# Cross-attention on one core: the first loads exchanged between two DMA queues, one quarter of x2 loaded ahead of Wq and Wk, nine warming products for ten

## The chip, the core and the metric

The kernel runs on one NeuronCore of a Trainium2 chip. Five engines work side by side, each through its own list of instructions: TensorE (PE, with its weight loads shown apart as PEld), VectorE (DVE), ScalarE (ACT), GpSimd (POOL) and SyncE (SP). Loads from HBM are issued by SP, ACT or POOL and are carried out by 16 DMA engines that all of them share. The metric is the time of one execution on the device in microseconds; smaller is better. A time is given as the median of several runs.

## What is computed

Eight batches. For each, with x1 and x2 of 512 channels by 1024 positions:

```python
q = jnp.einsum('bcn,dc->bnd', x1, Wq) + bq
k = jnp.einsum('bcn,dc->bdn', x2, Wk) + bk[:, None]
v = jnp.einsum('bcn,dc->bdn', x2, Wv) + bv[:, None]
attn = jax.nn.softmax(jnp.einsum('bnd,bdm->bnm', q, k), axis=2)
attn_out = jnp.einsum('bcm,bnm->bcn', v, attn)
return attn_out + x1
```

Wq and Wk have 64 rows, Wv has 512. All is float32.

## The kernel before

**How exact products are made.** Most large products are not done in plain float32. An operand is split into a high part (`h`, rounded by the float32r type), a low part (`l`) and a mixed one (`d`); three cheap products with these parts are then summed. For Wv the parts are made by `wh`, `wl`, `wd` and `w4`, for a quarter of x2 (256 positions, called a chunk) by `xh`, `xl`, `xd`. A few products are done in plain float32, since there is no time to split yet: those of v for the first quarter of x2 (`VF`, line 366), and the projections to q and k (`Q` and `K`, through `project`, line 205).

**What sets the order.** Nothing is scheduled by the compiler: three tables of words, `FIRST`, `MIDDLE` and `LAST`, list every step of a batch, and `follow` issues them in that order. Each engine takes its own steps out of that one list, in order. `FIRST` holds batch 0 and parts of batch 1, `MIDDLE` is used for batches 1 to 6. Ahead of them stands `begin` (line 515).

**The head.** `begin` issues, alternately, four pieces of the first quarter of x2 (`hx`, lines 163 to 166, 128 KB each, from SP) and four pieces of Wv (`hw`, lines 168 to 171, 256 KB each, from ACT). While these are on their way PE runs products on a tile of zeros, in three groups of four, three and three (`ps_warm`, line 525), and ACT evaluates one exponential, before which its table is loaded (line 528). Then `FIRST` starts:

```python
VF.0.0 VF.1.0 VF.1.1 wh.0 VF.1.2 VF.1.3 wl.0 wd.0 w4.0 wh.1 wl.1 wd.1 w4.1 VF.0.1 VF.0.2 VF.0.3 lwq ldx2.0
ldx2.1 xh.1 lsd K xl.1 xh.2 xh.3 ldx1.0 bv ke xd.1 xl.2 xl.3 VX.2 ldx1.1 jf.0 xd.2 xd.3 sy.2 sy.3 sy.5 jf.1 Q
```

`VF.j.c` is one float32 product of block j with piece c of x2's first quarter and piece c of Wv. `lwq` loads Wq and Wk (one tile, `wqk_sb`, 256 KB) and then the two biases (`bqk_sb`, 1 KB). `ldx2.0` loads the second quarter of x2 (512 KB), `ldx2.1` the second half (1024 KB), `lsd` the bias of v, and each `ldx1` two pieces of x1 of 512 KB; all of these are issued by SP. `K` needs all of x2 and Wk: its products alternate between the first half of x2 and the second, piece by piece. `VX.2` comes right behind it on PE, then `Q`, which needs x1.

**How loads wait for one another.** The framework gives the loads that SP and ACT issue eight completion semaphores in turn (`DMAHW0` to `DMAHW7`). A load that takes a semaphore again waits until the load that had it before, the eighth before it in the order of issue, has landed. A queue issues in order, so whatever stands behind such a load waits with it.

Of the kernel before, what the change touches and what calls it, by code (L numbers as in the profile page):

```python
# [10 lines left out]
FR = mybir.dt.float32r  # L11
AF = mybir.ActivationFunctionType
ALU = mybir.AluOpType
# [10 lines left out]
T = 4096.0  # L24
SPLIT = 1.0 - 2.0**-13
# [2 lines left out]


FIRST = """  # L30
VF.0.0 VF.1.0 VF.1.1 wh.0 VF.1.2 VF.1.3 wl.0 wd.0 w4.0 wh.1 wl.1 wd.1 w4.1 VF.0.1 VF.0.2 VF.0.3 lwq ldx2.0
ldx2.1 xh.1 lsd K xl.1 xh.2 xh.3 ldx1.0 bv ke xd.1 xl.2 xl.3 VX.2 ldx1.1 jf.0 xd.2 xd.3 sy.2 sy.3 sy.5 jf.1 Q
kc VY.2 VY.3 qe kr cy.2 cy.3 vh.0 qd kl jn.2 vl.0 qr sy.4 VX.3 jn.3 vh.1 VX.4 VY.5 cy.5 vd.0 VX.5 VY.4 cy.4 ql
S.0.0 S.0.1 S.0.2 S.0.3 S.0.5 Sc.0.0 Sc.0.1 Sc.0.2 Sc.0.3 S.0.4 Sc.0.4 Sc.0.5 S.0.6 Sc.0.6 S.0.7 Sc.0.7 S.1.1
# [48 lines left out]
def kernel(  # L83
# [12 lines left out]
    nc = tc.nc  # L96
    P = 128
    B, N, C = x1T.shape
    D = wqk.shape[3]
    CT = C // P  # L100
    MT = N // P
    H = 512
    QN = 256
# [8 lines left out]
    bqk_sb = const.tile([P, 2], F32, name="bqk_sb")  # L112
# [4 lines left out]
    wraw, wtmp = {}, {}  # L117

    BUFS = {"X": 3, "Y": 3, "sc": 2, "raw": 2, "top": 2, "kh": 5, "kl": 5, "kd": 4, "es": 2, "few": 2, "r": 2, "y": 2, "o": 3, "x": 2}

    LATE = (6, 7)

    def f32(t):
        return t.bitcast(F32)

    def new(shape, tag, name, dtype=F32):
        return sb.tile(shape, dtype, tag=tag, name=name, bufs=BUFS.get(tag, 1))

    def bank(tag, name):
        return psum.tile([P, H], F32, tag=tag, name=name, bufs=BUFS[tag])  # L130

    class Batch:
# [30 lines left out]
        def hx(self, c):  # L163
            if c == 0:
                self.x2[0] = new([P, 2, CT, QN], "x", "x2_0_0")
            nc.sync.dma_start(self.x2[0][:, 0, c, :], x2[0, :, 0, c])

        def hw(self, c):
            if c % 2 == 0:
                wraw[c // 2] = new([P, 2, C], "kd", f"w_raw{c // 2}")  # L170
            nc.scalar.dma_start(wraw[c // 2][:, c % 2, :], wvT[c])

        def lwq(self):
            nc.sync.dma_start(wqk_sb, wqk)
            nc.sync.dma_start(bqk_sb, bqk)

        def lsd(self):
            nc.sync.dma_start(seed, bv.broadcast_to([P, C]))
# [168 lines left out]
        def chunk(self, k):  # L347
            return self.x2[k // 2][:, k % 2]

        def xh(self, k):  # L350
            self.c[k] = {"h": new([P, CT, QN], "kh", f"xh_{self.b}_{k}", FR)}
            nc.scalar.activation(self.c[k]["h"], self.chunk(k), AF.Copy, scale=-SPLIT)

        def xl(self, k):
            self.c[k]["l"] = new([P, CT, QN], "kl", f"xl_{self.b}_{k}", FR)
            nc.vector.tensor_tensor(self.c[k]["l"], self.chunk(k), f32(self.c[k]["h"]), ALU.add)

        def xd(self, k):
            c = self.c[k]
            c["d"] = new([P, CT, QN], "kd", f"xd_{self.b}_{k}", FR)  # L360
            nc.vector.scalar_tensor_tensor(c["d"], f32(c["l"]), T, f32(c["h"]), ALU.mult, ALU.add)

        def VF(self, j, c):
            if c == 0:
# [101 lines left out]
        def late(self, u):  # L466
            return u in LATE and not self.final

# [46 lines left out]
    def begin():  # L515
        for c in range(CT):
            states[0].hx(c)
            states[0].hw(c)
        nc.vector.memset(warm, 0.0)
        nc.vector.memset(spark, 0.0)  # L520

        for i, times in enumerate((4, 3, 3)):
            ps = bank("Y", f"ps_warm{i}")
            for k in range(times):
                nc.tensor.matmul(
                    ps, warm, warm.unsqueeze(1).to_broadcast([P, 4, P]), start=(k == 0), stop=(k == times - 1)
                )
        nc.scalar.activation(spark, spark, AF.Exp)
# [10 lines left out]
    with tc.manual_schedule():  # L539
        begin()  # L540
        follow(FIRST, 0)
        for b in range(1, B - 1):
            follow(MIDDLE, b)
        follow(LAST, B - 1)
# [31 lines left out]
```

## Time and profile before

| what | value |
|---|---|
| median of 3 runs | 660.87 us (660.82 to 661.15) |
| the profiled execution | 661.69 us |
| its span, first to last instruction | 659.9 us |
| PE busy | 652.8 us, 99% of the span |
| DVE, ACT, POOL busy | 619.0, 452.4, 203.5 us |
| read from HBM, written to it | 51.91 MB, 16.78 MB |

The span covers the program's instructions; 1.8 us of the profiled execution lie around it. PE is busy nearly from end to end, so what can change is, above all, when it starts on useful work and where it still waits. The page's list of waits gives PE's own waits: 1.4 us for a load of x ahead of `K`, 1.0 us at the very start, 0.8 us and 0.2 us later for ACT.

### The profile page before, as it was taken

What the parts mean: (1) busy time and instruction counts of PE and PEld (TensorE: products, weight loads), DVE (VectorE), ACT (ScalarE), POOL (GpSimd) and SP (SyncE); (2) the same over time, 40 slices, a digit from 0 to 9 for tenths busy, and PEclk for the clock granted to TensorE, in tenths of its full rate; (3) what the DMA queues carried; (4) which work ended last, traced back from release to release, by engine and by line L of the source; (5) the groups of instructions that cost most, each with busy time, mean ns of one, the idle gap of its engine ahead of it and who ended that gap; (6) DMA issues with size and microseconds to landing.
All of it is one profiled execution on the core that took longest, in us unless ns stands there. A gap on an engine that the chain in (4) does not pass through costs nothing.

```text
span 659.9 us, 8059 instructions
## 1 busy us (share of the span) xinstructions
PE 652.8 (99%) x2802; PEld 492.4 (75%) x2802; DVE 619.0 (94%) x689; ACT 452.4 (69%) x670; POOL 203.5 (31%) x162
## 2 busy tenths in 40 slices
PE   8999999999999999999999999999999999999997
PEld 3664888677886688866888668886688776887886
DVE  4789999999999999999999999999999999999994
ACT  5688676876587675876767757677675975759542
POOL 0014432323414333043520335212352214412451
PEclk9999999999999999999999999999999999999999
DMA  8534648364665647474563745737367275632374
GB/s 316 191 96 107 119 98 221 73 201 96 129 175 112 175 98 163 124 173 120 114 173 96 216 100 111 173 83 224 81 128 179 77 207 98 126 81 49 93 150 124
DMA packets 41464, 90.21 MB, mean 137 GB/s; under 512 B 13136, under 2 KB 13904, under 8 KB 37712
## 3 DMA queue, kind: packets, MB, share of 16 engines
q0 software_dynamic: 13536, 33.04, 30.0%
q1 hardware_dynamic: 27312, 55.62, 25.4%
q10 hardware_dynamic: 576, 1.05, 0.4%
q8 instruction: 22, 0.36, 0.2%
q14 instruction: 18, 0.15, 0.1%
HBM read 51.91 MB, written 16.78 MB: 104 GB/s over the span
## 4 chain that ended last, share of the span: by engine, by line
PE 96%; DMA 2%; ACT 1%; DVEq 0%; issue 0%; ACTq 0%; DVE 0%
PE ps_oX L426 34%; PE ps_oY L426 17%; PE ps_vX L386 17%; PE ps_s L262 9%; PE ps_vY L386 8%; PE ps_k L205 4%; PE ps_q L205 4%; PE ps_o L451 2%; DMA x<-in_x_dram 1%; DMA w_raw<-in_wvT_dram 1%; ACT eh L297 0%; ACT e L293 0%; ACT ps_vY L382 0%; ACT vy L401 0%; ACT es L312 0%; ACT vh L408 0%
## 5 line engine op out<-in xcount | busy, mean ns | idle before, releaser
L426 PE MATMUL ps_oY<-vd,ed 128*128 128x512 f32 x496 | 193.2, 392 | 0.0
L426 PE MATMUL ps_oX<-vh,eh 128*128 128x512 f32 x496 | 193.0, 389 | 0.0
L426 PE MATMUL ps_oX<-vl,el 128*128 128x512 f32 x496 | 193.0, 389 | 0.0
L426 PEld LDWEIGHTS ps_oY<-vd,ed 128*128 128x128 f32 x496 | 93.1, 188 | 25.0 <-issue 5.1
L506 POOL DMA_DIRECT2D o<-in_x1T_dram x62 | 55.6, 916 | 171.6 <-ACT o L503 97.6
L426 PEld LDWEIGHTS ps_oX<-vl,el 128*128 128x128 f32 x496 | 93.1, 188 | 19.5
L426 PEld LDWEIGHTS ps_oX<-vh,eh 128*128 128x128 f32 x496 | 93.1, 188 | 19.3 <-issue 0.2
L293 ACT ACTIVATE e<-e 128x1024 f32<-128x1024 f32 x64 | 67.9, 1062 | 49.6 <-DVE e L290 48.3
L267 ACT COPY e<-ps_s 128x512 f32<-128x512 f32 x128 | 70.9, 589 | 28.6 <-PE ps_s L262 27.6
L329 POOL PARTITION_ALL_REDUCE den<-es x32 | 80.7, 2522 | 26.0 <-DVE es L319 25.0
L306 DVE SCALAR_TENSOR_TENSOR ed<-el,eh 128x1024 fp32r<-128x1024 f32 x62 | 83.0, 1341 | 2.1
L315 POOL DMA_DIRECT2D es<-e x32 | 28.6, 895 | 179.1 <-ACT es L312 166.9
L301 DVE TENSOR_TENSOR el<-e,eh 128x1024 fp32r<-128x1024 f32 x62 | 79.5, 1298 | 0.0
L290 DVE TENSOR_TENSOR e<-e,top 128x1024 f32<-128x1024 f32 x64 | 77.0, 1231 | 0.0
L282 POOL PARTITION_ALL_REDUCE top<-max x32 | 46.9, 1466 | 68.0 <-DVE max L278 67.9
L386 PE MATMUL ps_vX<-wh,xh 128*128 128x512 f32 x248 | 67.6, 394 | 0.0
L386 PE MATMUL ps_vY<-wd,xd 128*128 128x512 f32 x248 | 65.9, 393 | 0.8 <-ACT ps_vY L382 0.8
L386 PE MATMUL ps_vX<-wl,xl 128*128 128x512 f32 x248 | 66.3, 389 | 0.0
L297 ACT ACTIVATE eh<-e 128x1024 fp32r<-128x1024 f32 x62 | 64.6, 1054 | 0.5
L401 ACT COPY vy<-ps_vY 128x512 f32<-128x512 f32 x62 | 36.4, 591 | 40.0 <-PE ps_vY L386 38.8
L386 PEld LDWEIGHTS ps_vX<-wh,xh 128*128 128x128 f32 x248 | 45.8, 188 | 15.7 <-DVE max L277 4.1
L386 PEld LDWEIGHTS ps_vY<-wd,xd 128*128 128x128 f32 x248 | 46.2, 188 | 12.5 <-ACT ps_vY L382 1.6
(59 smaller groups left out, 963.5 us busy)
## 6 DMA issues: line engine op xcount, KB each, us to landing
x<-in_x_dram SPq DMA_DIRECT2D x29, 1024.0 KB, 6.6
es<-e POOLq DMA_DIRECT2D x32, 512.0 KB, 4.6
out_dram<-o SPq DMA_DIRECT2D x63, 256.0 KB, 2.4
o<-in_x1T_dram POOLq DMA_DIRECT2D x62, 256.0 KB, 4.3
x<-in_x_dram SPq DMA_DIRECT2D x5, 512.0 KB, 10.3
k<-k SPq DMA_DIRECT2D x16, 128.0 KB, 2.2
q<-q SPq DMA_DIRECT2D x16, 128.0 KB, 2.4
w_raw<-in_wvT_dram ACTq DMA_DIRECT2D x4, 256.0 KB, 4.1
```

Of the source, the lines that this page charges most:

```text
L205: nc.tensor.matmul(ps[r, :], wqk_sb[:, which, c, :], x(h, c), start=(c == 0), stop=(c == CT - 1))
L262: nc.tensor.matmul(ps, k[:, ts(i, P)], self.qa[:, ts(h, H)], start=(z == 0), stop=(z == 1))
L267: nc.scalar.copy(self.half[h][:, :, i, :], self.ps[h, i].rearrange("p (q n) -> p q n", q=2))
L290: nc.vector.tensor_tensor(e, e, top, ALU.subtract)
L293: nc.scalar.activation(self.unit(u), self.unit(u), AF.Exp)
L297: nc.scalar.activation(self.e[u]["h"], self.unit(u), AF.Copy, scale=SPLIT)
L301: nc.vector.tensor_tensor(self.e[u]["l"], self.unit(u), f32(self.e[u]["h"]), ALU.subtract)
L306: nc.vector.scalar_tensor_tensor(e["d"], f32(e["l"]), -T, f32(e["h"]), ALU.mult, ALU.add)
L329: nc.gpsimd.partition_all_reduce(self.den[Q], self.es[Q][:, 0, :], P, ReduceOp.add)
L386: nc.tensor.matmul(ps, self.c[j // 2][z][:, c, ts(j % 2, P)], w[z][:, c, :], start=(start and c == 0), stop=(stop and c == CT - 1), skip_g ...
L426: nc.tensor.matmul(ps, self.e[u][z][:, m, :], self.v[m // 2][z][:, m % 2, :], start=start, stop=stop, skip_group_check=True,)
L506: nc.gpsimd.dma_start(self.o[u], x1T[self.b, ts(u, P), :], accum_op=ALU.add)
```

## The change

Four things in the head of the program; every other step keeps its place.

- The pieces of x2's first quarter (`hx`) are issued by ACT, the pieces of Wv (`hw`) by SP.
- `ldx2.0` stands ahead of `lwq` in `FIRST`.
- The two biases leave `lwq` and are issued by ACT, right behind the pieces of x2.
- Nine warming products in three groups of three, for ten.

The functions `xh`, `xl` and `xd` now take the part of a chunk that `apart` gives. With `WHOLE = 2` its condition compares a chunk's number with 0.5, which no whole number equals, so that part is always the whole chunk and these instructions keep their shape of 128x1024.

```diff
@@ -28,7 +28,7 @@
 
 
 FIRST = """
-VF.0.0 VF.1.0 VF.1.1 wh.0 VF.1.2 VF.1.3 wl.0 wd.0 w4.0 wh.1 wl.1 wd.1 w4.1 VF.0.1 VF.0.2 VF.0.3 lwq ldx2.0
+VF.0.0 VF.1.0 VF.1.1 wh.0 VF.1.2 VF.1.3 wl.0 wd.0 w4.0 wh.1 wl.1 wd.1 w4.1 VF.0.1 VF.0.2 VF.0.3 ldx2.0 lwq
 ldx2.1 xh.1 lsd K xl.1 xh.2 xh.3 ldx1.0 bv ke xd.1 xl.2 xl.3 VX.2 ldx1.1 jf.0 xd.2 xd.3 sy.2 sy.3 sy.5 jf.1 Q
 kc VY.2 VY.3 qe kr cy.2 cy.3 vh.0 qd kl jn.2 vl.0 qr sy.4 VX.3 jn.3 vh.1 VX.4 VY.5 cy.5 vd.0 VX.5 VY.4 cy.4 ql
 S.0.0 S.0.1 S.0.2 S.0.3 S.0.5 Sc.0.0 Sc.0.1 Sc.0.2 Sc.0.3 S.0.4 Sc.0.4 Sc.0.5 S.0.6 Sc.0.6 S.0.7 Sc.0.7 S.1.1
@@ -118,6 +118,8 @@
 
     BUFS = {"X": 3, "Y": 3, "sc": 2, "raw": 2, "top": 2, "kh": 5, "kl": 5, "kd": 4, "es": 2, "few": 2, "r": 2, "y": 2, "o": 3, "x": 2}
 
+    WHOLE = 2
+
     LATE = (6, 7)
 
     def f32(t):
@@ -163,16 +165,15 @@
         def hx(self, c):
             if c == 0:
                 self.x2[0] = new([P, 2, CT, QN], "x", "x2_0_0")
-            nc.sync.dma_start(self.x2[0][:, 0, c, :], x2[0, :, 0, c])
+            nc.scalar.dma_start(self.x2[0][:, 0, c, :], x2[0, :, 0, c])
 
         def hw(self, c):
             if c % 2 == 0:
                 wraw[c // 2] = new([P, 2, C], "kd", f"w_raw{c // 2}")
-            nc.scalar.dma_start(wraw[c // 2][:, c % 2, :], wvT[c])
+            nc.sync.dma_start(wraw[c // 2][:, c % 2, :], wvT[c])
 
         def lwq(self):
             nc.sync.dma_start(wqk_sb, wqk)
-            nc.sync.dma_start(bqk_sb, bqk)
 
         def lsd(self):
             nc.sync.dma_start(seed, bv.broadcast_to([P, C]))
@@ -347,18 +348,26 @@
         def chunk(self, k):
             return self.x2[k // 2][:, k % 2]
 
+        def apart(self, k):
+
+            return slice(P, QN) if self.first and k == WHOLE / 2 - 0.5 else slice(0, QN)
+
         def xh(self, k):
+            at = self.apart(k)
             self.c[k] = {"h": new([P, CT, QN], "kh", f"xh_{self.b}_{k}", FR)}
-            nc.scalar.activation(self.c[k]["h"], self.chunk(k), AF.Copy, scale=-SPLIT)
+            nc.scalar.activation(self.c[k]["h"][:, :, at], self.chunk(k)[:, :, at], AF.Copy, scale=-SPLIT)
 
         def xl(self, k):
-            self.c[k]["l"] = new([P, CT, QN], "kl", f"xl_{self.b}_{k}", FR)
-            nc.vector.tensor_tensor(self.c[k]["l"], self.chunk(k), f32(self.c[k]["h"]), ALU.add)
+            c, at = self.c[k], self.apart(k)
+            c["l"] = new([P, CT, QN], "kl", f"xl_{self.b}_{k}", FR)
+            nc.vector.tensor_tensor(c["l"][:, :, at], self.chunk(k)[:, :, at], f32(c["h"][:, :, at]), ALU.add)
 
         def xd(self, k):
-            c = self.c[k]
+            c, at = self.c[k], self.apart(k)
             c["d"] = new([P, CT, QN], "kd", f"xd_{self.b}_{k}", FR)
-            nc.vector.scalar_tensor_tensor(c["d"], f32(c["l"]), T, f32(c["h"]), ALU.mult, ALU.add)
+            nc.vector.scalar_tensor_tensor(
+                c["d"][:, :, at], f32(c["l"][:, :, at]), T, f32(c["h"][:, :, at]), ALU.mult, ALU.add
+            )
 
         def VF(self, j, c):
             if c == 0:
@@ -516,10 +525,11 @@
         for c in range(CT):
             states[0].hx(c)
             states[0].hw(c)
+        nc.scalar.dma_start(bqk_sb, bqk)
         nc.vector.memset(warm, 0.0)
         nc.vector.memset(spark, 0.0)
 
-        for i, times in enumerate((4, 3, 3)):
+        for i, times in enumerate((3, 3, 3)):
             ps = bank("Y", f"ps_warm{i}")
             for k in range(times):
                 nc.tensor.matmul(
```

## The prediction, made before the changed kernel was run

> **What bounds the kernel now.** I read the page first, then the chain that ended last, then PE's timeline of the head, and last the loads one by one. The page:
>
> ```profile
> span 659.9 us, 8059 instructions
> PE 652.8 (99%) x2802; PEld 492.4 (75%) x2802; DVE 619.0 (94%) x689; ACT 452.4 (69%) x670; POOL 203.5 (31%) x162
> PE 96%; DMA 2%; ACT 1%; DVEq 0%; issue 0%; ACTq 0%; DVE 0%
> ```
>
> PE is the bound. The last row, the chain's shares, gives DMA 2% of the span, some 13 us, and the chain in order of time says where these lie:
>
> ```profile
> 1.17 4.39 DMA w_raw<-in_wvT_dram
> 5.57 8.90 DMA x<-in_x_dram
> 14.51 3.65 PE ps_k L205 x14
> 18.16 2.04 PE ps_vX L386 x8
> 20.20 3.58 PE ps_q L205 x16
> ```
>
> They are all ahead of 14.51 us. The load of x that was issued at 5.57 us and took 8.90 us is the second half of x2; it lands at 14.47 us, and K goes on 0.04 us later. From there on PE's work follows without a break in these rows. So the kernel's time is 14.5 us of head and 645 us behind it, and a head that is a microsecond shorter takes a microsecond off the whole, as long as nothing else becomes late.
>
> What PE does before:
>
> ```profile
> 0.98 4.03 PE L525 MATMUL ps_warm<-warm 128*128 128x512 bf16 x10 [0.98 <-DVE spark L520]
> 4.84 7.24 PE L366 MATMUL ps_v<-w_raw,x 128*128 128x512 f32 x16
> 8.39 0.30 PEld L366 LDWEIGHTS ps_v<-w_raw,x 128*128 128x128 f32 x2 [0.77 <-DMA w_raw<-in_wvT_dram]
> 12.02 1.07 PE L205 MATMUL ps_k<-x,wqk_sb 128*64 128x512 f32 x2
> 14.51 3.65 PE L205 MATMUL ps_k<-x,wqk_sb 128*64 128x512 f32 x14 [1.42 <-DMA x<-in_x_dram]
> ```
>
> The VF products run from 4.84 us to 12.08 us, held up once by the last piece of Wv. K's first product (two passes) ends at 13.09 us, and then PE stands still for 1.42 us. Whatever brings the VF products forward only lengthens this stand, unless the second half of x2 lands earlier. That landing is the one number to forecast.
>
> **The change part by part.** The issue order of SP, before. `x_0_0` is the first half of x2 of batch 0, `x_0_1` the second, `w_raw` Wv; `DMAHW` are the completion semaphores:
>
> ```order
> L166 DMA x_0_0_74<-in_x_dram 128x256 x4
> L174 DMA wqk_sb<-in_wqk_dram 128x512
> L175 DMA bqk_sb<-in_bqk_dram 128x2 [waits DMAHW1_49]
> L161 DMA x_0_0_74<-in_x_dram 128x1024 [waits DMAHW2_49]
> L161 DMA x_0_1_124<-in_x_dram 128x2048 [waits DMAHW3_49]
> L178 DMA bv_seed<-in_bv_dram 128x512 [waits DMAHW4_49]
> ```
>
> And with the change:
>
> ```order
> L173 DMA w_raw_76<-in_wvT_dram 128x512 x2
> L173 DMA w_raw_81<-in_wvT_dram 128x512
> L173 DMA w_raw_81<-in_wvT_dram 128x512 [waits DMAHW0_49]
> L163 DMA x_0_0_74<-in_x_dram 128x1024 [waits DMAHW1_49]
> L176 DMA wqk_sb<-in_wqk_dram 128x512 [waits DMAHW2_49]
> L163 DMA x_0_1_123<-in_x_dram 128x2048 [waits DMAHW3_49]
> L179 DMA bv_seed<-in_bv_dram 128x512 [waits DMAHW4_49]
> ```
>
> The last piece of Wv now stands in SP's queue, ahead of the second quarter of x2; Wq and Wk, which waited for nothing, now wait for a landing, behind that quarter. The second half of x2 still has the same place and the same semaphore. ACT's list, before and then with the change:
>
> ```order
> L171 DMA w_raw_76<-in_wvT_dram 128x512 x2
> L171 DMA w_raw_81<-in_wvT_dram 128x512
> L171 DMA w_raw_81<-in_wvT_dram 128x512 [waits DMAHW0_49]
> L528 ACT_TABLE_LOAD
> L528 ACTIVATE spark<-spark 128x1 [waits DVE_49]
> L186 ACTIVATE wh<-w_raw_76 128x1024 [waits DMAHW3_49]
> ```
>
> ```order
> L168 DMA x_0_0_74<-in_x_dram 128x256 x4
> L528 DMA bqk_sb<-in_bqk_dram 128x2
> L538 ACT_TABLE_LOAD
> L538 ACTIVATE spark<-spark 128x1 [waits DVE_49]
> L187 ACTIVATE wh<-w_raw_76 128x1024 [waits DMAHW3_49,DMAHW1_49]
> ```
>
> No load in ACT's list waits any longer, so the table load no longer stands behind one.
>
> *Issue and landing.* Starts and times to landing (the loads' own rows, one window each; in the order of issue the first and second pieces of Wv and of x2, Wq with Wk, the last piece of Wv, x2's second quarter, its second half):
>
> ```profile
> 0.73 1.80 SPq L166 DMA_DIRECT2D x<-in_x_dram  x4
> 2.58 0.43 SPq L174 DMA_DIRECT2D wqk_sb<-in_wqk_dram  x1
> w_raw<-in_wvT_dram ACTq DMA_DIRECT2D x1, 256.0 KB, 3.8
> x<-in_x_dram SPq DMA_DIRECT2D x1, 128.0 KB, 3.6
> w_raw<-in_wvT_dram ACTq DMA_DIRECT2D x1, 256.0 KB, 4.4
> x<-in_x_dram SPq DMA_DIRECT2D x1, 128.0 KB, 3.9
> wqk_sb<-in_wqk_dram SPq DMA_DIRECT2D x1, 256.0 KB, 5.1
> w_raw<-in_wvT_dram ACTq DMA_DIRECT2D x1, 256.0 KB, 3.8
> 5.12 0.80 SPq L161 DMA_DIRECT2D x<-in_x_dram  x2
> x<-in_x_dram SPq DMA_DIRECT2D x1, 512.0 KB, 6.8
> x<-in_x_dram SPq DMA_DIRECT2D x1, 1024.0 KB, 8.9
> ```
>
> The first two pieces land at 0.73 + 3.8 = 4.5 us (Wv) and 0.73 + 3.6 = 4.3 us (x2); the second ones, issued at 1.17 us as the chain's first row shows for Wv, at 5.6 and 5.1 us. With the change SP issues the last piece of Wv at 4.3 us, when x2's first piece has landed, 0.2 us sooner than now; then the second quarter of x2 at about 4.8 us (5.12 now), Wq and Wk at 5.2 us, and the second half at about 5.65 us, when Wv's second piece has landed and SP has issued three loads of some 0.4 us each since 4.3 us. That is 0.1 us later than now, which is nothing against 8.9 us to landing: the load waits for bytes, not for its issue.
>
> *Bytes.* Through the second half of x2 the rows sum to 4 x 128 + 4 x 256 + 256 + 512 + 1024 KB, with 1 KB of biases 3.41 MB, before as after; term one is **0**. What the 16 DMA engines did meanwhile:
>
> ```profile
> 0.00:2.50 2.50, 1.52 (x4) 0.58 (x5) 0.12 (x2) 0.00 (x0) 0.19 (x4) 1.00 0.10 22
> 2.50:6.00 3.50, 3.50 (x10) 1.51 (x9) 0.00 (x0) 1.08 (x1) 0.00 (x0) 1.00 0.98 340
> 6.00:7.50 1.50, 1.50 (x5) 0.65 (x4) 0.10 (x1) 1.35 (x3) 0.00 (x0) 1.00 1.07 374
> 7.50:9.00 1.50, 1.50 (x5) 0.49 (x4) 1.47 (x2) 0.34 (x1) 0.00 (x0) 1.00 1.06 322
> 9.00:12.20 3.20, 3.20 (x9) 1.25 (x8) 2.36 (x3) 1.91 (x3) 0.00 (x0) 1.00 0.91 349
> 0.00:12.20 12.20, 11.22 (x27) 4.47 (x28) 4.05 (x6) 4.68 (x6) 0.19 (x4) 1.00 0.80 279
> 0.00:14.50 14.50, 12.11 (x28) 4.48 (x28) 5.54 (x7) 6.45 (x8) 0.19 (x4) 1.00 0.84 302
> ```
>
> (The last three columns are the granted clock, the DMA engines' busy share and GB/s.) From 2.5 us on they are busy without a gap, so an earlier issue alone gains nothing.
>
> *A gap where Wq and Wk were.* They filled the stage around 6 us; with the change the only bytes at hand then are the last of the first seven pieces and the last piece of Wv, issued at 4.3 us. If that piece needs its 3.8 us as now, it lands at 8.1 us, and with 0.26 MB less ahead of it the engines idle for up to 0.26 MB / 374 GB/s = 0.7 us; if it comes as soon as there is room, for 0. I take **+0.2 us**, nearer the lower end, since it is issued sooner than now and has the second quarter close behind it. At the very start 22 GB/s flow, with pieces of 128 KB in SP's queue; larger ones stand there now: from 0 to -0.3 us (a tenth of 2.5 us), **-0.1 us** taken.
>
> *Uneven engines.* By 12.20 us, 279 x 12.2 = 3.40 MB had been moved, all that the second half of x2 needs. By 14.50 us it was 302 x 14.5 = 4.38 MB, and only then had that half landed: for 2.3 us some engines worked on later loads while others were behind. They fell behind between 7.5 and 9 us, where the rate drops to 322 GB/s, just when the second quarter of x2 begins to move. With the change that quarter follows on Wv's last piece in one queue and Wq with Wk stands between it and the half. How uneven the engines come out of that, no row shows. Lower end: all of the 2.3 us but the time that a last packet needs to be reported, say -1.8 us. Upper end: +0.7 us, a third more. A later load of 1024 KB, issued alone at 25.81 us, shows that unevenness or waiting is no accident of the head:
>
> ```profile
> 25.81 0.53 SPq L148 DMA_DIRECT2D x<-in_x_dram  x1
> x<-in_x_dram SPq DMA_DIRECT2D x1, 1024.0 KB, 6.1
> ```
>
> At the 349 GB/s of the head it would take 3.0 us and, with the 2.5 us of the start-up, 5.5 us; it took 6.1 us. That is 0.6 us of unevenness, less than the head's 2.3. I take **-0.5 us**, a third of the way from the one to the other, as the access to x2 stays the same.
>
> *PE and ACT.* One product fewer: the weight loads of the last warming product and of the first VF stand at
>
> ```profile
> 4.37 0.14 PEld L525 LDWEIGHTS <-warm 128*128 128x128 bf16 x1 [0.28 <-issue]
> 4.63 0.41 PEld L366 LDWEIGHTS ps_v<-w_raw,x 128*128 128x128 f32 x2
> ```
>
> so VF starts 0.26 us earlier at most, not before 4.5 us, when its data are there. A sooner last piece of Wv removes up to 0.2 us from within VF. VF then ends at about 11.6 us. ACT:
>
> ```profile
> 4.92 1.28 ACT L528 ACT_TABLE_LOAD   x1 [4.92 <-DMA w_raw<-in_wvT_dram]
> 6.33 1.04 ACT L186 ACTIVATE wh<-w_raw 128x1024 fp32r<-128x1024 f32 x1
> 14.49 2.01 ACT L352 ACTIVATE xh<-x 128x1024 fp32r<-128x1024 f32 x2 [0.54 <-DMA x<-in_x_dram]
> ```
>
> The table load starts near 3 us and `wh` at 5.6 us, 0.7 us sooner. All of it is taken up again by the wait for the second half of x2, which holds PE at 14.51 us and ACT at 14.49 us: worth **0** here, and 0.5 us more for each of the two if that cover were gone.
>
> *Sum:* 0 + 0.2 - 0.1 - 0.5 = **-0.4 us**. On the profiled execution that is 659.9 - 0.4 = 659.5 us of span, 661.3 us with what lies around it. It ran 0.8 us above the median, so against the median the forecast is 660.87 - 0.4 = **660.5 us**.
>
> A rule of the Trainium skill speaks against the exchange: "DMA: Bandwidth & Descriptors", section "Issuing engines are not separate DMA queues", has all queues end on the same 16 engines, so that another issuer saves only issue time. By that rule the sum would be 0 and the time 660.9 us, an estimate. The trace agrees in that the engines are busy throughout; that some of them lag by 2.3 us is outside the rule.
>
> **Rivals.** *The lag goes:* the second half lands near 12.7 us. K's first product would end near 12.7 us too (13.09 less 0.4), so this is the most there is to gain: -1.8 us, 659.1 us. For it: x2's second quarter starts sooner, and the lag arose where it met Wv's last piece. Against it: the same 512 KB are read in the same way. Chance 0.27. *The queue runs dry:* in the stage from 6.0 to 7.5 us Wq with Wk and the last piece of Wv, 0.52 MB, were moved, 1.4 us at 374 GB/s. If the last piece, alone in the queue, comes only when the earlier ones are done and takes 5 us (as Wq with Wk did), all behind it is late: +1.5 us, 662.4 us. It decides once that piece lands after 9.3 us. Against it: issue moves 0.2 us forward. Chance 0.13. *The change does nothing that counts:* the second half lands at 14.5 us again, 660.9 us; this lies within the forecast's own range.
>
> **How the numbers follow.** The forecast has the remaining 0.60, with its own range from 659.7 to 661.4 us. What a measurement of this kernel can tell from no change is about 0.2%, 1.3 us: under 659.55 us is faster, above 662.2 us slower. Faster 0.27, within 0.60, slower 0.13. The range is 659.0 to 661.9 us: it takes in the first rival's price and leaves out the second.
>
> **What would show it.** The chain of the changed kernel should have a load of x that ends between 13 and 15 us and K's 14 passes right behind it; VF should end near 11.6 us with no wait for Wv; the table load should start near 3 us; PE's wait ahead of K should grow to about 1.5 us. Landing of Wv's last piece near 8 us refutes the dry queue, after 9.3 us it confirms it. If K starts before 13 us, the lag is gone and my third term was too small. I am wrong altogether if the time behind K changes by more than 0.3 us: I count on that part to move as one piece.

## The result, and the profile after

| | median, us | runs | ratio to the kernel before, 95% interval |
|---|---|---|---|
| before | 660.87 (659.97 to 662.00) | 20 | |
| with the change | 661.95 (661.39 to 662.51) | 20 | 1.0015 [1.0008, 1.0022] |

The forecast was 660.5 us. The change costs 1.1 us where 0.4 us less was expected. That is less than the 0.2% (1.3 us) which the prediction called the bound, but with this many runs the interval leaves 1 out.

The two profiled executions differ by less: 661.65 us now (span 659.8) against 661.69 (659.9). Equal spans hide two things of about one microsecond each. The first shows in the chain that ended last, in order of time, of the changed kernel (start, length, what):

```profile
1.17 4.15 DMA x<-in_x_dram
5.34 0.33 SPq L176
5.71 7.58 DMA x<-in_x_dram
13.33 3.65 PE ps_k L206 x14
16.98 2.05 PE ps_vX L395 x8
```

The second half of x2 took 7.58 us instead of 8.90, and K's fourteen passes start at 13.33 us instead of 14.51: PE leads the execution before by 1.18 us. PE's timeline of the head says the same (start, busy, group, idle time ahead of it):

```profile
0.98 4.02 PE L535 MATMUL ps_warm<-warm 128*128 128x512 bf16 x9 [0.98 <-DVE spark L530]
4.79 7.21 PE L375 MATMUL ps_v<-w_raw,x 128*128 128x512 f32 x16
11.94 1.07 PE L206 MATMUL ps_k<-x,wqk_sb 128*64 128x512 f32 x2
```

In these two executions the head did what was hoped, and more. The second thing is in PE's list of waits (in all, times, longest), where the kernel before has no such row:

```profile
PE ps_s L263 <- DVE kl L256: 0.7, 1, 0.7
```

Once in the whole execution PE waits for `kl`, the low part of k, on VectorE (`kh` is the high part; `e` are the exponentials with their parts `el` and `ed`, `es` their partial sums, and `den` the sum of these over the partitions, which GpSimd makes). It is where batch 1 passes into batch 2. Here is that place in the timeline after the change, ACT, then DVE, POOL and PE:

```profile
152.93 2.20 ACT L294 ACTIVATE e<-e 128x1024 f32<-128x1024 f32 x2 [1.54 <-DVE e L291]
155.48 1.05 ACT L313 COPY es<-e 128x1024 f32<-128x1024 f32 x1 [0.35 <-ACT e L294]
156.44 1.05 ACT L252 ACTIVATE kh<-k 128x1024 fp32r<-128x1024 f32 x1
157.00 0.42 DVE L320 TENSOR_TENSOR es<-es 128x256 f32<-128x256 f32 x1
157.53 2.36 DVE L256 TENSOR_TENSOR kl<-k,kh 128x1024 fp32r<-128x1024 f32 x1
157.53 1.99 POOL L330 PARTITION_ALL_REDUCE den<-es  x1
158.82 0.39 PE L263 MATMUL ps_s<-qa,kh 128*128 128x512 f32 x1
159.94 0.50 PE L263 MATMUL ps_s<-qa,kl 128*128 128x512 f32 x1 [0.74 <-DVE kl L256]
```

And the same place before:

```profile
156.33 1.05 ACT L312 COPY es<-e 128x1024 f32<-128x1024 f32 x1
157.28 1.05 ACT L251 ACTIVATE kh<-k 128x1024 fp32r<-128x1024 f32 x1
158.13 0.42 DVE L319 TENSOR_TENSOR es<-es 128x256 f32<-128x256 f32 x1
158.46 1.22 DVE L255 TENSOR_TENSOR kl<-k,kh 128x1024 fp32r<-128x1024 f32 x1
158.65 2.69 POOL L329 PARTITION_ALL_REDUCE den<-es  x1
159.60 2.12 DVE L306 SCALAR_TENSOR_TENSOR ed<-el,eh 128x1024 fp32r<-128x1024 f32 x1
159.94 0.39 PE L262 MATMUL ps_s<-qa,kh 128*128 128x512 f32 x1
160.17 0.39 PE L262 MATMUL ps_s<-qa,kl 128*128 128x512 f32 x1
```

Read it from the top. ACT stands idle for 0.35 us ahead of the copy `es`, behind nothing but its own last exponential; nothing else in the trace holds it there. So `kh` comes later against VectorE's work than before, and `kl`, which needs `kh`, does too. Before, `kl` starts 0.33 us after the joining `es` (158.13, 158.46) and 0.19 us ahead of POOL's reduction `den`, and takes 1.22 us; the operation that `den` slows there is the next one, `ed`, which takes 2.12 us (1.21 with the change), and PE's list of waits has no row for it. Now both start at 157.53 us, and `kl` takes 2.36 us, 1.14 more. PE's product with `kl` would have followed 0.23 us behind the one with `kh`, at 159.05 us; it starts at 159.94, 0.9 us late. Of the lead of 1.18 us on the execution before, 159.94 - 160.17 = 0.2 us are left, and 0.1 at the end of the span.

Two questions were open: whether this one collision is the loss, and why ACT idles there. The change touches nothing near 155 us.

### The profile page after: what moved, and what is told of

Its sections match the earlier page's. It is cut to its first block, busy times and chain, and to the rows that moved or that the text cites. A ratio compares the mean times of both kernels' runs of the same rounds, so it can differ in the third digit from the quotient of the medians.

```text
span 659.8 us, 8058 instructions
## 1 busy us (share of the span) xinstructions
PE 653.1 (99%) x2801; PEld 492.5 (75%) x2801; DVE 619.8 (94%) x689; ACT 452.6 (69%) x670; POOL 201.1 (30%) x162
## 4 chain that ended last, share of the span: by engine, by line
PE 87%; DVE 8%; DMA 2%; ACT 1%; issue 1%; DVEq 0%; ACTq 0%; SPq 0%
PE ps_oX L435 31%; PE ps_oY L435 16%; PE ps_vX L395 15%; PE ps_s L263 8%; PE ps_vY L395 7%; PE ps_k L206 4%; PE ps_q L206 4%; PE ps_o L460 2%; DMA x<-in_x_dram 2%; DVE e L291 1%; DVE vl L422 1%; DVE vd L427 1%; DVE el L302 1%; DVE ed L307 1%; DVE v L413 1%
## 5 line engine op out<-in xcount | busy, mean ns | idle before, releaser
L395 PEld LDWEIGHTS ps_vY<-wd,xd 128*128 128x128 f32 x248 | 46.2, 188 | 12.4 <-ACT ps_vY L391 1.6
```

What stands on the lines that cost most here:

```text
L395: nc.tensor.matmul(ps, self.c[j // 2][z][:, c, ts(j % 2, P)], w[z][:, c, :], start=(start and c == 0), stop=(stop and c == CT - 1), skip_g ...
```

## The experiments

Each kernel was run beside the kernel before on the same chip; a ratio is to those runs. `K at` is the start of K's last fourteen passes (or, where K ran through, of its third pass) in the profiled execution, `kl` the length of the operation at batch 1's end.

| kernel | median, us | runs | ratio to before, 95% interval | span | K at | kl |
|---|---|---|---|---|---|---|
| b_again | 661.05 | 11 | 1.0002 [0.9994, 1.0011] | 658.6 | 13.17 | 1.22 |
| a_again | 662.00 | 12 | 1.0017 [1.0009, 1.0026] | 660.0 | 13.51 | 2.36 |
| swap_only | 663.06 | 9 | 1.0035 [1.0023, 1.0047] | 660.8 | 14.12 | 2.37 |
| order_only | 660.88 | 11 | 0.9999 [0.9990, 1.0008] | 659.4 | 14.02 | 1.22 |
| after_plus1 | 660.41 | 12 | 0.9993 [0.9984, 1.0001] | 658.9 | 13.38 | 1.22 |
| before_plus2 | 662.18 | 11 | 1.0015 [1.0007, 1.0024] | 660.4 | 13.93 | 2.37 |
| before_plus1 | 660.92 | 11 | 0.9995 [0.9987, 1.0004] | 659.5 | 14.03 | 1.22 |
| after_bqk_sp | 660.10 | 11 | 0.9986 [0.9978, 0.9995] | 658.0 | 12.26 | 1.22 |
| after_a3late | 660.37 | 11 | 0.9985 [0.9976, 0.9994] | 658.4 | 12.94 | 1.23 |
| swap_plus1 | 661.75 | 11 | 1.0006 [0.9997, 1.0014] | 660.1 | 14.70 | 1.22 |
| bqk_sp_ten | 660.32 | 11 | 0.9983 [0.9975, 0.9992] | 658.1 | 13.07 | 1.22 |
| nine_only | 661.45 | 11 | 1.0000 [0.9991, 1.0009] | 658.0 | 12.95 | 1.22 |

The kernel before had medians of 660.94, 661.46 and 661.33 us in the three groups of four, so the ratios are safer to compare across groups than the medians. Where K ran through, its sixteen passes end up to 0.5 us sooner than the column `K at` suggests: at 17.19 us in order_only, 16.30 in nine_only, 16.25 in bqk_sp_ten and 15.79 in after_bqk_sp, against 18.16 in the execution before and 16.98 in that of the changed kernel.

**Is the head's lead real, and which part brings it?** Theory A: the lead of the changed kernel is real, and it is lost where `kl` meets `den`. Theory B: there is no lead; the execution of before that was profiled had a slow head. The kernel before and the changed one were run once more, unedited, and with them two parts of the change alone. For b_again:

> The kernel before, unchanged, profiled once more. In the two profiles at hand K resumes at 14.51 us before and at 13.33 us with the change, 1.18 us sooner, yet both spans are 659.8 to 659.9 us: the lead is gone at 160 us, where the VectorE operation kl takes 2.36 us with the change and 1.22 us before, beside a GpSimd reduction (den) that starts in the same 10 ns. Theory A (the lead is real and is lost again where kl meets that reduction): K resumes near 14.5 us here too, kl of batch 2 takes 1.2 us, time near 660.9 us. Theory B (the head of the kernel before was caught on a slow execution; there is no lead): K resumes near 13.3 us here, and the span is near 659.1 us.

For a_again:

> The changed kernel, unchanged, profiled once more. Theory A: K resumes near 13.3 us, kl of batch 2 takes 2.4 us beside den, time near 661.9 us. Theory B: K resumes anywhere from 13 to 15 us, and the loss of 1.1 us lies in another place or is not there.

For swap_only, the exchange of the queues with the biases on ACT:

```diff
-            nc.sync.dma_start(self.x2[0][:, 0, c, :], x2[0, :, 0, c])
+            nc.scalar.dma_start(self.x2[0][:, 0, c, :], x2[0, :, 0, c])
...
-            nc.scalar.dma_start(wraw[c // 2][:, c % 2, :], wvT[c])
+            nc.sync.dma_start(wraw[c // 2][:, c % 2, :], wvT[c])
...
-            nc.sync.dma_start(bqk_sb, bqk)
...
+        nc.scalar.dma_start(bqk_sb, bqk)
```

> The exchange of the queues and the biases on ACT's queue alone; Wq and Wk still ahead of x2's second quarter, ten warming products. Theory A: K resumes between 13.3 and 14.5 us, and the time follows from whether kl of batch 2 takes 1.2 us (then 660.9 us less the lead) or 2.4 us (then up to 662 us). Theory B: time within 0.4 us of the kernel before, since no part of the change has a lead to lose.

For order_only, the second quarter of x2 ahead of Wq and Wk:

```diff
-VF.0.0 ... VF.0.3 lwq ldx2.0
+VF.0.0 ... VF.0.3 ldx2.0 lwq
```

> Only x2's second quarter ahead of Wq and Wk; queues and ten warming products as before. Theory A: the same as for the exchange alone: the lead of K, whatever it is, decides nothing by itself, the length of kl in batch 2 does, so 660 us with a short kl and up to 662 us with a long one. Theory B: within 0.4 us of the kernel before.

Both theories were half right. In b_again K goes on at 13.17 us although nothing was edited, so the 14.51 us that the prediction started from was one draw of a head that varies by more than a microsecond; and b_again keeps its lead to the end (658.6 us of span, 1.3 less), while a_again, as far ahead at 13.51 us, loses it at the same place as the changed kernel. The 663.06 us of swap_only lie above the 662 us that theory A allowed for. The slow `kl` is in the changed kernel, in a_again and in swap_only, and in neither execution of before nor in order_only. What the three share is ACT's list: two instructions more ahead of the place, the issue of the biases and one more semaphore wait (the one ahead of `wh`, which now waits for two loads).

**What makes ACT idle?** ACT's records in the trace, counted from 0 with its DMA issues and semaphore waits, show where that copy stands:

```
before         188 155.200 EVENT_SEMAPHORE   189 156.330 COPY es
after          190 154.073 EVENT_SEMAPHORE   191 155.483 COPY es
after_plus1    191 154.107 EVENT_SEMAPHORE   192 155.240 COPY es
before_plus2   190 154.641 EVENT_SEMAPHORE   191 156.054 COPY es
before         318 260.754 EVENT_SEMAPHORE   319 262.167 COPY es
```

A copy that is number 191 begins 1.41 us behind the start of its wait, any other here 1.13. The last line is a copy of the next batch in the kernel before: number 319 = 191 + 128, and it has the same idle time, where nothing on VectorE is close enough to collide:

```profile
262.17 1.06 ACT L312 COPY es<-e 128x1024 f32<-128x1024 f32 x1 [0.35 <-ACT e L293]
```

So theory C: every 128th record something costs ACT 0.3 us, hidden under the instruction in progress unless the first one behind the boundary follows on a wait. Its rival D: the exchange of the queues is slower as such. If C holds, one instruction more or less cures or spoils any variant. One further exponential of one column in the changed kernel, two in the kernel before, one there as a control, and, in the changed kernel, the biases taken off ACT:

```diff
         nc.scalar.activation(spark, spark, AF.Exp)
+        nc.scalar.activation(spark, spark, AF.Exp)
```

For after_plus1:

> The changed kernel with one more tiny exponential (128x1) on ScalarE at the start, so every later ScalarE instruction stands one place further on. What is known: the unchanged kernel profiled again resumed K at 13.17 us (not 14.51) and kept that lead to the end, span 658.6 us; in all three profiles with the exchanged queues ScalarE's copy es.3 of batch 1 starts 0.32 us after everything it waits for, and kl then collides with den. In those that copy is ScalarE's instruction 191 of the trace; in the kernel before the same 0.32 us appear at instruction 319, 128 later. Theory C (a block boundary in ScalarE's instruction stream every 128 instructions costs 0.32 us where a wait stands right ahead of it; the exchange moves the boundary onto es.3 by adding two ScalarE instructions): es.3 is instruction 192, no stall, kl takes 1.2 us, time 660.6 to 661.1 us, 1 us below the changed kernel. Theory D (the exchange as such, through the loads and their semaphores, brings about the late copy): stall and long kl remain, 661.9 us.

For before_plus2 (two such lines):

> The kernel before, with two more tiny exponentials on ScalarE at the start: no load, queue, semaphore or TensorE instruction is touched. Theory C: es.3 of batch 1 becomes ScalarE's instruction 191, stands 0.32 us, kl takes 2.4 us, time 661.8 to 662.1 us, 1 us slower than before. Theory D: no stall, kl 1.2 us, 660.9 us.

For before_plus1:

> The kernel before with one more tiny exponential: the control for the two. Theory C: es.3 is instruction 190, no stall, 660.9 us. Theory D: 660.9 us as well. If it is 1 us slower like the kernel with two, it is the added work at the start and not the place in the stream.

For after_bqk_sp:

```diff
         def lwq(self):
             nc.sync.dma_start(wqk_sb, wqk)
+            nc.sync.dma_start(bqk_sb, bqk)
...
-        nc.scalar.dma_start(bqk_sb, bqk)
```

> The changed kernel with the biases issued by SyncE again, behind Wq and Wk: ScalarE has one instruction fewer. Theory C: es.3 is instruction 190, no stall, kl 1.2 us, 660.6 to 661.2 us. Theory D: the exchanged queues are still there, 661.9 us.

The idle time and the length of `kl` came out as C has them in all four. The times of after_plus1 and after_bqk_sp, 660.41 and 660.10 us, lie below the ranges that C had given (from 660.6 us on); after_bqk_sp has a further reason, told below. That the period is 128 rests on two places, 191 and 319. The kernel before, with two instructions on 128 elements added in the first 6 us, has the whole picture at 158 us, ACT, DVE and POOL in turn:

```profile
156.05 1.06 ACT L312 COPY es<-e 128x1024 f32<-128x1024 f32 x1 [0.36 <-ACT e L293]
158.10 2.37 DVE L255 TENSOR_TENSOR kl<-k,kh 128x1024 fp32r<-128x1024 f32 x1
158.10 2.00 POOL L329 PARTITION_ALL_REDUCE den<-es  x1
```

It is 1.3 us slower than with one added (662.18, 660.92). The changed kernel, with one instruction more to execute, loses the idle time, `kl` is short again, and it runs in 660.41 us, 1.5 us less than without (by the ratios, 1.0015 against 0.9993):

```profile
155.24 1.06 ACT L313 COPY es<-e 128x1024 f32<-128x1024 f32 x1
157.37 1.22 DVE L256 TENSOR_TENSOR kl<-k,kh 128x1024 fp32r<-128x1024 f32 x1
157.56 2.69 POOL L330 PARTITION_ALL_REDUCE den<-es  x1
```

**Is it the idle time or the collision? And what is each part worth without it?** In after_a3late ACT's list stays as in the changed kernel; only `a3.2`, the joining that lets `den` start, is moved behind `kl`, in the table for batches 1 to 6:

```diff
-d.4 a3.2 R.4.0 R.4.1 +kr +kl +S.0.0 +S.0.1 ...
+d.4 R.4.0 R.4.1 +kr +kl a3.2 +S.0.0 +S.0.1 ...
```

> The changed kernel with one step moved in the table for batches 1 to 6: the last joining of the third quarter's sums (a3.2, VectorE, 0.42 us, on which the partition reduction den of POOL waits) stands behind kl instead of ahead of kr and kl. ACT's list is untouched, so the 0.3 us of idle ahead of the fourth quarter's es copy of batch 1 must still be there. Theory C with the collision as the price: kl starts ahead of den whatever ACT does, keeps 1.22 us, PE waits for it at most 0.4 us instead of 0.74, and the time falls to 660.4 to 661.2 us (ratio to the kernel before 0.9990 to 1.0000). If the late ACT itself is the price and the slow kl only comes along with it: 661.7 to 662.2 us, as the changed kernel. If taking kl early costs den something that matters: above 662.2 us.

The idle time is there as before, and `kl` is not slowed:

```profile
155.05 1.05 ACT L313 COPY es<-e 128x1024 f32<-128x1024 f32 x1 [0.36 <-ACT e L294]
157.09 1.23 DVE L256 TENSOR_TENSOR kl<-k,kh 128x1024 fp32r<-128x1024 f32 x1 [0.44 <-ACT kh L252]
158.23 0.42 DVE L320 TENSOR_TENSOR es<-es 128x256 f32<-128x256 f32 x1
158.75 2.69 POOL L330 PARTITION_ALL_REDUCE den<-es  x1 [1.46 <-DVE es L320]
```

VectorE now stands idle for 0.44 us, `den` meets an `el` at 159.78 us instead (2.04 us), PE's list of waits has no row for `kl`, and the kernel takes 660.37 us, a ratio of 0.9985 where 0.9990 to 1.0000 was expected. The 0.35 us of ACT cost nothing that can be seen by themselves; the price is the order in which `kl` and `den` start.

swap_plus1 is swap_only with one further exponential, bqk_sp_ten is after_bqk_sp with ten warming products, nine_only the kernel before with nine.

For swap_plus1:

> The exchange of the two queues alone (Wq and Wk ahead of x2's second quarter, ten warming products, biases on ACT), with one further exponential of 128x1 on ACT, which moves the fourth quarter's es copy of batch 1 from row 191 to row 192. Theory C: no idle ahead of that copy, kl 1.22 us, and the time falls by 0.9 to 1.4 us from the 663.06 us of the exchange alone, to 661.6 to 662.2 us; what is left above the kernel before (0.2 to 0.7 us) is the exchange's own price in the head. Theory D, the exchange as such is slower: still 662.8 to 663.3 us. If the exchange as such gains: under 660.8 us.

For bqk_sp_ten:

> The changed kernel with the biases issued by SP behind Wq and Wk, and ten warming products again for nine. If the product taken away is worth its 0.26 us (VF's start goes from 4.8 to 5.1 us) and nothing covers it: 660.3 to 660.5 us against the 660.10 us with nine. If the load of x2's second half covers it: 660.0 to 660.2 us. If ten products open the clock's gate sooner: under 660.0 us.

For nine_only:

> The kernel before with nine warming products for ten and nothing else. Its K waits 1 us and more for the second half of x2, so VF's start 0.26 us sooner should be covered: 660.7 to 661.1 us, ratio 0.9995 to 1.0005. If the clock's gate opens later for it and VF runs at half rate for longer than the cover: above 661.3 us. ACT's rows are as before, so no idle ahead of the es copy of batch 1 and kl 1.22 us.

With the copy shifted, the exchange alone comes down from a ratio of 1.0035 to 1.0006, and what is left is no gain (1.0006 [0.9997, 1.0014]). The product taken away is worth nothing that can be seen, in either pair (1.0000 for nine_only; 0.9986 and 0.9983 with nine and ten); the 0.26 us that were asked about are 0.0004 and less than these intervals can show. The 661.45 us of nine_only lie above the 660.7 to 661.1 us expected, but the kernel before took 661.33 us beside it. Nor is the new order of loads alone a gain: its second half of x2 lands early, but the last piece of Wv, still issued by ACT, comes late and holds VF up:

```profile
5.05 3.60 PE L366 MATMUL ps_v<-w_raw,x 128*128 128x512 f32 x8
9.91 3.70 PE L366 MATMUL ps_v<-w_raw,x 128*128 128x512 f32 x8 [1.27 <-DMA w_raw<-in_wvT_dram]
13.54 2.79 PE L205 MATMUL ps_k<-x,wqk_sb 128*64 128x512 f32 x12
```

This execution loses 0.4 us more far behind the head, at 118.43 us, where PE waits for ACT a second time; its list of waits, and then that of the kernel before, have

```profile
PE ps_vY L386 <- ACT ps_vY L382: 1.0, 2, 0.7
PE ps_vY L386 <- ACT ps_vY L382: 0.8, 1, 0.8
```

Whether that belongs to the order of loads or to this one execution was not tried.

Together, with nine products, they gain: the order sends x2 earlier, and with the exchange Wv's last piece stands ahead of it in the same queue. Without the slow `kl` that is 0.9993 [0.9984, 1.0001] in after_plus1, whose interval still takes in 1, and 0.9985 [0.9976, 0.9994] in after_a3late, 0.5 to 1.0 us.

after_bqk_sp, bqk_sp_ten and after_a3late are each faster than both kernels, by 0.9 to 1.1 us against before; between the three, nothing can be told.

## Why the prediction was wrong

**The step that failed** is its last: "I count on that part to move as one piece." The part behind K did not. In the profiled executions a lead of 1.18 us became 0.1 us, nearly all of it at one product at 159.94 us. From the end of K to the end of the span it takes 641.8 to 641.9 us in the eight executions without slow `kl` or any other loss, and 642.8 to 643.1 us in the four in which PE waits for `kl` (641.8 before, 642.9 with the change: 1.1 us, where the prediction called 0.3 its limit); in order_only and after_bqk_sp it takes 642.2. By the timed runs the collision costs 1.3 us (before_plus2 against before_plus1), 1.5 us (the changed kernel against after_plus1) or 1.9 us (the exchange alone, the two ratios). Each of the three is uncertain by 0.7 to 1.0 us either way, so the 1.0 us of the profiles fits them; whether it is the whole price stays open. The bounds that the prediction gave came from the head alone, and the price lay 140 us behind it. Its order listing showed both additions to ACT's list, the biases' load and a second semaphore for `wh` to wait for, and it put no price on them.

The terms of the sum came out near the sizes given, one of them by luck. These rows are windows of the changed kernel (its last three columns are the granted clock, the DMA engines' busy share and GB/s):

```profile
0.00:2.50 2.50, 1.52 (x4) 0.58 (x5) 0.12 (x2) 0.00 (x0) 0.19 (x4) 1.00 0.20 43
2.50:6.00 3.50, 3.50 (x9) 1.63 (x8) 0.00 (x0) 2.26 (x3) 0.00 (x0) 1.00 1.02 353
6.00:7.50 1.50, 1.50 (x4) 0.59 (x4) 1.18 (x1) 0.29 (x1) 0.00 (x0) 1.00 1.03 361
7.50:9.00 1.50, 1.50 (x5) 0.73 (x4) 1.27 (x2) 1.42 (x2) 0.00 (x0) 1.00 0.76 203
9.00:12.20 3.20, 3.20 (x8) 1.17 (x8) 2.45 (x2) 1.91 (x3) 0.00 (x0) 1.00 0.99 406
w_raw<-in_wvT_dram SPq DMA_DIRECT2D x1, 256.0 KB, 3.2
```

- *Start-up, -0.1 us:* 43 GB/s instead of 22 in the first 2.5 us, some 0.05 MB sooner; at 350 GB/s, 0.15 us.
- *A gap, +0.2 us:* there is one, later than expected. From 7.5 to 9 us the engines are busy for 0.76 of the time, 0.36 us of idling that the kernel before doesn't have. Wv's last piece, issued at 4.25 us, landed 3.2 us later, at 7.5 us, so the queue did not run dry for it; the rival of 662.4 us came near the time for a reason that is not its own.
- *Uneven engines, -0.5 us:* this term carries the head, and its size depends on the execution. From the completion records of the 16 engines for the second half of x2, all fourteen profiled executions:

| order in the queues | first engine done, us | last engine done, us | between them, us |
|---|---|---|---|
| before, b_again, before_plus1, before_plus2, nine_only | 11.7 to 12.0 | 14.5, 13.1, 14.0, 13.9, 12.6 | 2.5, 1.3, 2.3, 1.9, 0.9 |
| swap_only, swap_plus1 | 11.8, 12.1 | 14.1, 14.7 | 2.3, 2.6 |
| after, a_again, after_plus1, after_a3late | 11.7 to 11.8 | 13.3, 13.5, 13.3, 12.9 | 1.4, 1.7, 1.7, 1.1 |
| order_only, after_bqk_sp, bqk_sp_ten | 11.4 to 11.8 | 12.4, 12.1, 12.2 | 0.6, 0.7, 0.7 |

The first engine is done at about the same time whatever the order; the landing is set by how far the others lag. The mean landing is 13.6 us in the first row and 13.2 in the third, 0.4 us sooner: the size of the forecast, by luck, since it was taken against a single execution at the late end of its row; and with five and four executions that differ by 1.9 and 0.6 us among themselves, 0.4 us between the means is not shown to be more than chance. In the last row the two loads of x2 are issued 1.4 us apart or more, with the biases between them, against 0.4 us in the first two rows and 1.1 us in the third; that this keeps the engines even was not tried by itself. In after_bqk_sp and bqk_sp_ten another thing differs: the biases no longer take one of the eight semaphores ahead of Wv's last piece, which is issued at 2.1 us and not at 4.25; no run separates the two. The rival in which the lag goes is what after_bqk_sp shows, with K waiting for no load, and it brings 0.9 us there, not the 1.8 that the late execution of before suggested.

- *The signs:* the load of x ends at 13.29 us with K's fourteen passes behind it, VF has no wait for Wv, the table load starts at 3.10 us: as forecast. VF ends at 12.0 us, not 11.6: its sixteen passes start at 4.79 us, and take 7.21 us, the first 0.61 us where the others take 0.43. The trace's first record of the granted clock begins at 5.15 us here; in the fourteen executions it begins between 3.87 and 6.85 us, with nine products as with ten, and where it begins last, in before_plus1, the first two passes take 0.85 and 0.82 us. The forecast had no term for this. PE's wait ahead of K is 0.33 us, not 1.5, since the half landed 1.2 us sooner than in the execution before, not 0.4.

The rule of the Trainium skill that the prediction weighed ("DMA: Bandwidth & Descriptors", section "Issuing engines are not separate DMA queues"), that another issuer saves only issue time, agrees with what the exchange alone shows once its collision is gone: 1.0006, no gain.

## What to carry to other kernels

In a kernel whose order is written out by hand, one instruction added to an engine's list in the head can decide a race a hundred microseconds later: compare PE's list of waits before and after for a row that is new, and look for idle time that nothing releases. Where VectorE and GpSimd are started by the same event, put the operation that TensorE waits for ahead of it by order, not by a margin of 0.2 us. And take the head from several profiled executions: here it varied by 1.9 us under one order of loads, more than any edit moved it.

## What had not been expected of the hardware

- An operation of VectorE with two inputs beside a partition reduction on GpSimd takes 2.36 us instead of 1.22 when it starts 0 to 5 ns behind it (four executions), and 1.22 when it starts 0.19 us ahead of it (nine executions). The reduction takes 1.99 us in the first case and 2.69 in the second; how long it takes alone can't be told, since in the traces before, after and after_a3late every `den` overlaps some operation of VectorE. The Trainium skill has this rule in "SBUF — State Buffer", section "Who interferes with whom": a VectorE instruction with two inputs in SBUF and a GpSimd instruction that reads SBUF contend for a shared read port, and the order of issue decides which of them blocks. The trace agrees on the order. The page also calls the shared ports an exclusive lock; here `kl` is held up for 1.14 us, less than the 1.99 us of the reduction beside it, by the profile's spans, which are rough on GpSimd.
- ACT loses 0.35 us at its records 191 and 319. That the place in the list decides it was shown from both sides; that the copy waits for instructions to be loaded is only argued. For it speaks a row of the changed kernel's DMA queues:

```profile
q14 instruction: 18, 0.15, 0.1%
```

Eighteen packets of 0.15 MB in all are 8 KB each, which is 128 instructions if one has 64 bytes. And one of them moves with the list: where the copy is record 191, a packet of this queue starts 0.64 to 0.67 us behind the start of the copy (five executions); where it is record 192, that packet starts 4.1 us ahead of the copy, at 151.1 us (after_plus1) and 152.4 us (swap_plus1). So a load of instructions belongs to this place, but it starts behind the late copy, and what the copy itself waits for stays open. The Trainium skill, "Runtime: NRT & Kernel Launch", section "Instruction fetch mechanics", has blocks of 16 KiB, or 256 instructions, whose loading is mostly hidden. The first differs from this row; the second holds here except behind a wait.
